# A cross-network kernel: half-size loads and earlier squares, and a block of its own for one difference of the first chunk pair

## The chip, the cores and the metric

The kernel runs on one core of a Trainium2 chip. The metric is the device time of one execution in microseconds (us). All data are float32.

## What is computed

The reference is a compressed interaction network of three layers over x (1024 examples, 64 fields, 16 embedding columns):

```python
for i in range(3):
    z = jnp.einsum('bfe,bge->bfge', x0, h)          # all products of a field with a row of h
    y = jnp.einsum('oc,bce->boe', Ws[i], z.reshape(Bn, f0 * fh, e)) + bs[i][None, :, None]
    x_i, h = (y[:, :64], y[:, 64:]) if i != 2 else (y, y)
    xs.append(x_i)
pooled = jnp.sum(jnp.concatenate(xs, axis=1), axis=2)
return pooled @ fc_w.T + fc_b
```

Everything after the second half of the first layer is linear in what it multiplies, so the kernel folds the last layer and the output weights into small matrices ahead of the main loop. What remains for each example and column is two quadratic forms of x: h, the second half of the first layer, and q, a folded form of the third and second. Their product, and a few linear terms, are summed.

## The kernel before, in words

**Tiling.** The batch is cut into 32 chunks of 32 examples, so a chunk has N = 32 x 16 = 512 columns. Fields lie on partitions. The products x_f x_g of a chunk come in 4 quarters j of 4 tiles i; a tile is 128 products x 512 columns, and a quarter, 128 x 2048, fills one of 14 SBUF blocks named z. A quarter is made by one VectorE product of xa (SBUF) with xp, a PSUM copy that ScalarE makes of the loaded xb (`second`, L563). A plain chunk contracts its 16 tiles with both weight matrices wh (for h) and wq (for q).

**Pairs.** Chunks 0 to 3 are the head, chunks 4 and 5 follow as plain chunks, 30 and 31 (and the q half of 2 and 3) end the kernel as plain ones. The other 24 chunks go in 12 pairs (n = 0 to 11, k = n + 3). A pair's two chunks a and b are multiplied by the two weight matrices in a scheme that needs seven runs of matmuls instead of eight, at the price of sums and differences. Each run has seven tiles, in two rows j = 0 (4 tiles) and j = 1 (3 tiles). The operands are X and B21 (products of chunk a), B22 and T3 (products of chunk b, T3 from the sum that `w_both`, L649, makes), and three differences that GpSimd makes, row by row (`w_mix`, L654): first T2 = T3 - X, then T3 = B22 - T2 in place, then T2 = T2 - B21 in place. Row j = 1 of T2 overwrites row 1 of X: its block is `p["X"][1]` (L657). Six of these GpSimd operations belong to a pair, on 128 x 2048 (row 0) or 128 x 1536 (row 1) elements.

**Windows.** TensorE works on one pair per window. The runs go into three PSUM banks: alpha in one half of the array's columns, delta and beta in the other. `window` (L738) writes the order out by hand as two columns of jobs that `zipped` (L530) interleaves, so that a job of one half runs beside a job of the other. Column one: the run X into alpha, jobs left over from the pair before (`first_fill`, 3 jobs), the run T2 into alpha, `second_fill` (2 jobs, and those handed over), the run T3 into alpha, 2 more jobs. Column two: the run T3 into delta, `late_run` of the pair before (10 jobs), the run B21 into beta, and the negative run, T2 (after its second difference) into delta. Of that last run the final `p["late"]` jobs are handed over to the next window: two from the first pair, then one and two in turn. Windows after the first read X row 1 ahead of row 0. The window of the first pair (n = 0, "window 0") is filled with jobs left of chunks 4 and 5 and with empty places (None). `squares` (L731) ends each window with four matmuls of 64 x 64.

**Order.** All is emitted in the order of times given to `at` (L527); T0 = 33 is window 0, SPAN = 31 the distance of windows, in places of TensorE's list and not in us. Each engine then works its own list in that order, and waits on semaphores where data or a buffer isn't ready. VectorE's list about window 0: X row 1 and B21 row 0 of the first pair (L645), `factors` of chunks 0 and 1 (L287 and L288: the second multiplies hb by a snapshot, both in SBUF, into uu), a sum (L299), B21 row 1, the products of the second pair up to its X row 1, among them `factors` of chunks 4 and 5 (L290), then the second pair's B21. Blocks z are handed out by `take` from a list of vacant ones, first freed first taken, each with a number of uses.

**Loads.** All loads are issued by SyncE in the same order. `load_e` (L160) brings x of a chunk to 128 partitions (the 64 fields twice), `square` (L169) squares the upper half in place on ScalarE. `h_extra` (L577) reads the squares, `v0x` (L584) the lower half, `q_extra` (L572) both. The first four chunks to be treated so are 4, 5, 0 and 1: loaded at 0, squared at 22, read at 28.1. `load_wx` (L542) loads two weight tables of 1 MB at -0.2 and -0.1; GpSimd weighs them (L548), VectorE adds them up (L552) and ScalarE places them (L557, at 17.1 and 20.1).

Of the kernel before, what the change touches and what calls it, by code (L numbers as in the profile page):

```python
# [38 lines left out]
AF = mybir.ActivationFunctionType  # L39
# [3 lines left out]
F = 64  # L43
# [25 lines left out]
def cin_kernel(ctx, tc, xra, xrb, wh, w0r, w1h, w2t, wx1, wx0, vec, out):  # L69
    nc = tc.nc  # L70
# [6 lines left out]
    halves = [slice(0, F), slice(F, 128)]  # L77

    def const_tile(name, shape):
        return const.tile(shape, F32, tag=name, name=name)  # L80
# [4 lines left out]
    def take(uses=1):  # L85
        n = vacant.pop(0)
        left[n] = uses
        return n

    def used(n, times=1):  # L90
        left[n] -= times
        assert left[n] >= 0
        if left[n] == 0:
            vacant.append(n)
# [22 lines left out]
    for base in (0, 64, -64):  # L117
        nc.gpsimd.affine_select(
            out=shift, in_=shift, compare_op=ALU.not_equal, fill=1.0, base=base,
# [12 lines left out]
    va, vb, v0 = (const_tile(n, [128, F]) for n in ("va", "vb", "v0"))  # L132
# [6 lines left out]
    xas, xbs, xxs, es = {}, {}, {}, {}  # L139
# [19 lines left out]

    def load_e(c):  # L160
        es[c] = sp.tile([128, N], F32, tag="e", name=f"e_{c}", bufs=4)
        nc.sync.dma_start(out=es[c], in_=xra[c, 0:128])

    def load_xx(k):
        xxs[k] = sp.tile([128, N], F32, tag="xx", name=f"xx_{k}")
# [1 line left out]
            nc.sync.dma_start(out=xxs[k][halves[n]], in_=xra[2 * k + n, 0:F])  # L167

    def square(c):  # L169
        nc.scalar.activation(es[c][halves[1]], es[c][halves[1]], AF.Square)  # L170

    def load_chunk(c):
        load_xa(c)
# [200 lines left out]
    for h in range(2):  # L374
        at = slice(32 * h, 32 * h + 32)
# [38 lines left out]
    def m_ap(f1, f2, dims):  # L414
        return bass.AP(tensor=md.tensor, offset=md.offset + f1 * row + f2 * F, ap=dims)
# [3 lines left out]
    for half, queue in enumerate((nc.sync, nc.scalar)):  # L419
        queue.dma_start(  # L420
            out=m_ap(0, 32 * half, [[row, F], [1, 32 * F]]), in_=m_rows[halves[half]]
# [5 lines left out]
        out=m_ap(64, 68, [[row, 4], [4 * F, 7], [1, 4 * F]]),  # L427
        in_=m_rows[0:4, 4 * F :].rearrange("p (k c) -> p k c", c=4 * F),
# [98 lines left out]
    def at(when, fn, *args, **flags):  # L527
        ops.append((when, len(ops), fn, args, flags))

    def zipped(when, *columns):  # L530
        for n, column in enumerate(columns):
            for m, job in enumerate(column):
                if job is not None:
                    at(when + m + n / len(columns), *job)
# [99 lines left out]
    def w_run(p, out, w, name, start=False, at_t=0, order=GROUPS):  # L634
        return [
            (w_job, p, out, w, j * NI + i + at_t, name, start and n == 0)
            for n, (j, i) in enumerate(order)
        ]

    wh_all, wq_all = w_all[:, :, 0:64], w_all[:, :, 64:128]  # L640
    s1, s2, s3, s4, neg = (ws[:, n] for n in range(5))
# [12 lines left out]
    def w_mix(p, j, out, in0, in1):  # L654
        p.setdefault(out, {})
        if j not in p[out]:
            p[out][j] = take(9) if j == 0 else p["X"][j]  # L657
        o, x, y = p[out][j], p[in0][j], p[in1][j]
        tiles = slice(j, NI)
        nc.gpsimd.tensor_tensor(  # L660
            blocks[o][:, tiles], blocks[x][:, tiles], blocks[y][:, tiles], ALU.subtract
        )
        for b in (x, y):
            if b != o:
                used(b)
# [26 lines left out]
    def make_pair(t, p, when, mixed):  # L692
        a, b = p["a"], p["b"]
        for when, c, j, name, uses in (
            (when[0], b, 2, "B22", 5), (when[1], b, 0, None, 0), (when[2], b, 0, "T3", 9),
            (when[3], a, 0, "X", 5), (when[4], b, 3, "B22", 6), (when[5], b, 1, None, 0),
            (when[6], b, 1, "T3", 9), (when[7], a, 1, "X", 12), (when[8], a, 2, "B21", 5),
            (when[9], a, 3, "B21", 6),
        ):
            if name is None:  # L700
                at(t + when, w_both, p, j)
                continue
            if name != "T3":
                at(t + when - (3.3 if p["k"] > 4 and name == "B22" and j == 2 else 2.7), second, c, j)
            at(t + when, w_product, p, c, j, name, uses)
        for when, j, *names in zip(
            mixed, (0, 1, 0, 1, 0, 1), *zip(
                *(2 * (("T2", "T3", "X"),) + 2 * (("T3", "B22", "T2"),) + 2 * (("T2", "T2", "B21"),))
            )
        ):  # L710
            at(t + when, w_mix, p, j, *names)

    def first_fill(p):
        a = p["a"]
        return [
            (w_job, p, beta, wq_all, NI, "X"), (w_job, p, beta, wq_all, NT - NI, "B21"),
            (lambda: q_extra(a, va, p["beta"]),),
        ]

    def second_fill(p):  # L720
        return [
            (w_job, p, delta, wh_all, NI, "X"), (w_job, p, delta, wh_all, NT - NI, "B21"),
        ] + w_run(p, delta, neg, "T2")[-p["late"] :]

    def late_run(p):
        b = p["b"]
        return [
            (w_job, p, alpha, neg, NI, "T3"), (w_job, p, alpha, s4, NI, "B22"),
        ] + w_run(p, alpha, s4, "B22") + [(lambda: q_extra(b, vb, p["alpha"]),)]
# [8 lines left out]
    def window(t, p, fill, late, pad=[], order=GROUPS[4:] + GROUPS[:4]):  # L738
        zipped(
            t,  # L740
            w_run(p, alpha, wq_all, "X", True, order=order) + fill[0] + w_run(p, alpha, s2, "T2")
            + fill[1] + w_run(p, alpha, s1, "T3")
            + [(w_job, p, alpha, wh_all, NI, "T3"), (w_job, p, alpha, s1, NI, "B22")],
            w_run(p, delta, s3, "T3", True) + late
            + w_run(p, beta, wq_all, "B21", True, 2 * NI)
            + pad + w_run(p, delta, neg, "T2")[: -p["late"]],
        )
        at(t + 30.2, squares, p)
        at(t + 6.8, snap_p1, p)
        at(t + 6.9, snap_p7, p)  # L750
        at(t + 6.8 + len(fill[0]) + 7, snap_u2, p)

    def end_pair(t, p, whens):
        hb_, qa, uub, ha, uua, xv, add = whens
        at(t + hb_, w_hb, p)
        at(t + qa, w_qa, p)
        at(t + uub, w_uu, p, alpha, "A", snaps[2])
        at(t + ha, w_ha, p)
        at(t + uua, w_uu, p, delta, "O", snaps[0])
        at(t + xv, x_v0x, p["k"])  # L760
        at(t + add, sums, p["k"])


    def load_pair(t, p, b0, a0, b1, a1):
        a, b = p["a"], p["b"]
        at(t + b0, load_xa, b)
        at(t + b0, load_xb, b, 2, 0)
        at(t + a0, load_xa, a)
        at(t + a0, load_xb, a, 0)
        at(t + b1, load_xb, b, 3, 1)  # L770
        at(t + a1, load_xb, a, 1, 2, 3)
        for c in (b, a):
            at(t + 1, load_e, c)
            at(t + 14, square, c)
        at(t + 1.1, load_xx, p["k"])
# [5 lines left out]
    at(-0.1, load_wx, 1, wx1)  # L781
    for n in (4, 5, 0, 1):
        at(0, load_e, n)
        at(22, square, n)
    for n in (0, 2):
        at(0.1, load_xx, n)
    for v, fc, mul, add, put in ((0, fcr[:, 0:64], 4, 17, 17.1), (1, fcr[:, 64:128], 5, 20, 20.1)):
# [32 lines left out]
    for n in range(NPAIR):  # L820
        k = n + 3
        s = k % 2
        p = {
            "k": k, "A": halves[s], "O": halves[1 - s], "b": 2 * k + s, "a": 2 * k + 1 - s,
            "late": 2 - n % 2,
        }
        pairs.append(p)
        t = T0 + SPAN * n
        if n == 0:
            load_pair(t, p, -39.9, -33.3, -33.05, -27)  # L830
            make_pair(
                t, p, (-23.4, -20.7, -20.4, -17.8, -14.2, -11.5, -8.1, -1, 0.5, 3),
                (-5, 6.6, 7.2, 12.4, 16.4, 21.7),
            )
            left5 = [[(contract_half, 5, 3, i, n) for i in (2, 3)] for n in range(2)]
            window(
                t, p, ([left5[1][0], (q_extra, 4, va)], [left5[1][1]]),
                [left5[0][0], (q_extra, 5, va), None, None], [left5[0][1], None, None, None, None],
                GROUPS,
            )  # L840
        else:
            q = pairs[-2]
            load_pair(t, p, -34, -28, -27.8, -27.7)
            make_pair(
                t, p, (-21.4, -18.7, -18.4, -15.8, -12.2, -9.5, -6.1, -2, 1.6, 4.2),
                (-5, 2.8, 7.2, 12.4, 16.4, 21.7),
            )
            window(t, p, (first_fill(q), second_fill(q)), late_run(q))
            end_pair(t, q, (0.7, 11.7, 17.9, 22.3, 23.2, 24, 27.5))
# [45 lines left out]
    c, k = NCH - 1, NP - 1  # L895
    t, q = T0 + SPAN * NPAIR, pairs[-1]
# [3 lines left out]
    for n, when in ((2, t - 4), (3, t - 4), (c - 1, t), (c, t)):  # L900
        at(when, load_e, n)
        at(t + 12, square, n)
# [9 lines left out]
    for n in (2, 3, c - 1, c):  # L912
        at(t - 0.1 + (n > 3) * 22, new_acc, n)
    qs = [[(head_q_half, n, m) for m in range(NT)] for n in (2, 3)]
    zipped(
        t,
        first_fill(q) + second_fill(q) + qs[0] + [(q_extra, 2, va), (q_extra, c - 1, va, None, True)],
        qs[1][:3] + late_run(q) + qs[1][3:] + [(q_extra, 3, va), (q_extra, c, va, None, True)],
    )
# [128 lines left out]
```

## Time and profile before

The time before is 467.2 us, the median of 3 runs (467.14 to 468.12). The profiled execution spans 468.5 us.

| engine | busy us | share of the span |
|---|---|---|
| TensorE, matmuls (PE) | 459.3 | 98% |
| TensorE, weight loads (PEld) | 171.1 | 37% |
| VectorE (DVE) | 397.1 | 85% |
| ScalarE (ACT) | 114.9 | 25% |
| GpSimd (POOL) | 330.3 | 71% |

How to read it: in a timeline a row has the start in us from the begin of the span, the time it covers in us, the engine, the line of the kernel, the operation, out<-in by the program's names, and how many are merged. In brackets stands the idle time of the engine ahead of it and what ended that. In the list of waits a row has who waited for whom, then the us in total, how many times, and the longest. DMA moves 91.29 MB in all, a mean of 195 GB/s; in the stretch ahead of window 0, from 52 to 75 us, it runs without pause.

### The profile page before, as it was taken

To read this page: it belongs to the slowest core of one execution; us is meant where nothing else is said; L and a number is where in the kernel's file an instruction comes from. 1 tells how busy PE (TensorE), PEld (TensorE's weight loads), DVE (VectorE), ACT (ScalarE), POOL (GpSimd) and SP (SyncE) were. 2 spreads that over 40 slices of the span, in tenths; PEclk is the share of its full clock that TensorE was granted. 3 is DMA by queue.
4 is the path that set the end of the run, shared out by engine and by line. 5 is a ranking of instruction groups with operands and counts; after the bars stand their busy time and mean duration, and the time that the engine had idled before them with its cause. 6 is when DMAs were issued, how large, how long until landed. Compare 5 with 4: busy or idle time off the path is not lost.

```text
span 468.5 us, 6050 instructions
## 1 busy us (share of the span) xinstructions
PE 459.3 (98%) x2308; PEld 171.1 (37%) x2308; DVE 397.1 (85%) x283; ACT 114.9 (25%) x211; POOL 330.3 (71%) x99
## 2 busy tenths in 40 slices
PE   7999999998999999999999999999999999999997
PEld 4565343232333333333333333333333333355444
DVE  3995597998898998989898998989898998999621
ACT  2142211441222213131312313122311314222101
POOL 5323689189997979899797979989797979600000
PEclk9999999999999999999999999999999999999999
DMA  8986999694818375562827465471828656061000
GB/s 301 401 289 153 355 414 297 217 313 146 290 50 277 127 235 190 162 243 90 303 70 248 167 205 207 140 279 63 307 81 252 219 174 231 24 224 46 0 1 2
DMA packets 35297, 91.29 MB, mean 195 GB/s; under 512 B 6240, under 2 KB 6912, under 8 KB 30340
## 3 DMA queue, kind: packets, MB, share of 16 engines
q1 hardware_dynamic: 34212, 89.88, 56.0%
q10 hardware_dynamic: 1056, 1.02, 0.8%
q8 instruction: 18, 0.29, 0.3%
q14 instruction: 11, 0.09, 0.1%
HBM read 89.25 MB, written 1.64 MB: 194 GB/s over the span
## 4 chain that ended last, share of the span: by engine, by line
PE 74%; DVE 12%; issue 6%; DMA 4%; POOL 3%; ACT 1%; SPq 1%; POOLq 0%; DVEq 0%; ACTq 0%
PE alpha L537 41%; PE acc L537 11%; PE beta L537 6%; DVE z L645 6%; PE delta L537 6%; PE acc L253 6%; PE acc L271 3%; POOL z L660 2%; DMA z<-in_wx 2%; DMA z<-in_w0r 2%; DVE acc L299 1%; POOL z L548 1%; DVE uu L688 1%; DVE xp L651 1%; DVE uu L295 1%
## 5 line engine op out<-in xcount | busy, mean ns | idle before, releaser
L660 POOL TENSOR_TENSOR z<-z,z 128x2048 f32<-128x2048 f32 x72 | 286.7, 4031 | 39.5 <-PE alpha L537 27.7
L645 DVE TENSOR_TENSOR z<-xa,xp 128x2048 f32<-128x2048 f32 x96 | 216.7, 2280 | 13.2 <-POOL z L660 12.2
L537 PE MATMUL alpha<-z,ws 128*64 128x512 f32 x576 | 196.6, 592 | 0.0
L537 PE MATMUL delta<-z,ws 128*64 128x512 f32 x336 | 150.7, 594 | 1.2 <-POOL z L660 1.2
L565 ACT COPY xp<-xb 128x512 f32<-128x512 f32 x93 | 54.7, 590 | 222.1 <-DVE z L645 167.1
L537 PEld LDWEIGHTS alpha<-z,ws 128*64 128x64 f32 x576 | 61.5, 137 | 105.1 <-issue 103.8
L537 PE MATMUL beta<-z,w_all 128*64 128x512 f32 x216 | 96.9, 593 | 0.0
L537 PE MATMUL alpha<-z,w_all 128*64 128x512 f32 x192 | 86.9, 595 | 0.9 <-DVE z L645 0.9
L537 PE MATMUL acc<-z,w_all 128*64 128x512 f32 (+3 forms) x320 | 78.0, 509 | 0.0
L239 DVE TENSOR_TENSOR z<-xa,xp 128x2048 f32<-128x2048 f32 (+2 forms) x33 | 67.5, 2087 | 8.7 <-ACT xp L565 5.3
L537 PEld LDWEIGHTS delta<-z,ws 128*64 128x64 f32 x336 | 45.0, 137 | 14.2 <-issue 11.4
L537 PEld LDWEIGHTS alpha<-z,w_all 128*64 128x64 f32 x192 | 25.3, 137 | 58.2 <-issue 48.8
L537 PEld LDWEIGHTS acc<-z,w_all 128*64 128x64 f32 (+1 forms) x320 | 33.2, 147 | 34.9 <-issue 33.8
L537 PEld LDWEIGHTS beta<-z,w_all 128*64 128x64 f32 x216 | 28.9, 137 | 13.9 <-issue 13.9
L253 PE MATMUL acc<-z,w_all 128*64 128x256 f32 x256 | 29.1, 382 | 2.6 <-DVE z L239 2.4
L239 POOL TENSOR_TENSOR z<-xa,xb 128x2048 f32<-128x2048 f32 x4 | 18.1, 4558 | 19.1 <-DMA xb<-in_xrb 19.1
L253 PEld LDWEIGHTS acc<-z,w_all 128*64 128x64 f32 x256 | 18.0, 137 | 14.8 <-DVE z L239 4.0
L537 PE MATMUL delta<-z,w_all 128*64 128x512 f32 x48 | 22.6, 592 | 0.0
L290 DVE SCALAR_TENSOR_TENSOR uu<-acc,vs,snap 64x512 f32<-64x512 f32 (+2 forms) x5 | 3.2, 643 | 20.3 <-ACT snap L282 20.2
L299 DVE TENSOR_REDUCE acc<-uu 128x64 f32<-128x1024 f32 (+3 forms) x20 | 20.2, 1017 | 0.2
L170 ACT ACTIVATE e<-e 64x512 f32<-64x512 f32 x32 | 18.3, 620 | 4.4 <-DMA e<-in_xra 4.0
L537 PE MATMUL y<-e,v 64*64 64x512 f32 x64 | 17.9, 613 | 0.0
(98 smaller groups left out, 290.0 us busy)
## 6 DMA issues: line engine op xcount, KB each, us to landing
xa<-in_xra SPq DMA_DIRECT2D x32, 1024.0 KB, 4.7
xb<-in_xrb SPq DMA_DIRECT2D x128, 256.0 KB, 6.9
e<-in_xra SPq DMA_DIRECT2D x32, 256.0 KB, 3.5
xx<-in_xra SPq DMA_DIRECT2D x32, 128.0 KB, 2.5
z<-in_w2t SPq DMA_DIRECT2D x2, 1024.0 KB
z<-in_wx SPq DMA_DIRECT2D x2, 1024.0 KB, 9.3
z<-in_w1h SPq DMA_DIRECT2D x1, 1024.0 KB
xa<-in_xra SPq DMA_DIRECT2D x3, 256.0 KB
```

The lines of the kernel that those rows point to most:

```text
L170: nc.scalar.activation(es[c][halves[1]], es[c][halves[1]], AF.Square)
L239: engine.tensor_tensor(blocks[zs[c, j]][:, at, :], xas[c][:, at, :], xbs[c][j].unsqueeze(1).to_broadcast([128, last - first, N]), ALU.mult,)
L253: nc.tensor.matmul(accs[c][halves[n]], w_all[:, t, 0:64], blocks[zs[c, j]][:, i, n * H2 : (n + 1) * H2], start=(t == 0), stop=(j == last a ...
L271: nc.tensor.matmul(accs[c][halves[1 - c % 2]], w_all[:, t, 64:128], blocks[zs[c, j]][:, i, :], start=(t == 0), stop=False, skip_group_chec ...
L295: nc.vector.scalar_tensor_tensor(uu[:, to, :], ys[k], cx, xxs[k], ALU.add, ALU.mult)
L299: nc.vector.tensor_reduce(acc[rows, of, k, half], uu[rows, of if at is None else at, E * half.start : E * half.stop].rearrange("p k (b e) ...
L537: nc.tensor.matmul(out, w, rhs, start=start, stop=stop, skip_group_check=True)
L548: nc.gpsimd.tensor_tensor(w, w, fc.unsqueeze(1).to_broadcast([128, 32, F]), ALU.mult)
L565: nc.scalar.copy(bank, xbs[c][j])
L645: nc.vector.tensor_tensor(blocks[b], xas[c], xbs[c][j].unsqueeze(1).to_broadcast([128, NI, N]), ALU.mult)
L651: nc.vector.tensor_tensor(bank, bank, xbs[p["b"]][j], ALU.add)
L660: nc.gpsimd.tensor_tensor(blocks[o][:, tiles], blocks[x][:, tiles], blocks[y][:, tiles], ALU.subtract)
```

## The change

It has three parts. First, `load_e` loads x to 64 partitions alone, half the bytes, and `square` reads that half and writes the other; the first four squares are emitted at 18 instead of 22, which is ahead of the second placement (20.1). The first pair's last loads of chunk b (quarters 3 and 1) are issued ahead of the second weight table. Second, the first pair's row 1 of T2 takes a block of its own instead of overwriting X row 1, and is emitted at 1.5 instead of 6.6. Third, the first pair hands no job of its negative run over; from the second pair on two and one are handed over in turn, and the empty places at the end of window 0 go from four to one. The purpose of the first part is that the squares are there when TensorE wants them, of the second that GpSimd need not wait for TensorE's reads of X, and of the third to fill the places that this opens.

```diff
     def load_e(c):
         es[c] = sp.tile([128, N], F32, tag="e", name=f"e_{c}", bufs=4)
-        nc.sync.dma_start(out=es[c], in_=xra[c, 0:128])
+        nc.sync.dma_start(out=es[c][halves[0]], in_=xra[c, 0:F])
...
     def square(c):
-        nc.scalar.activation(es[c][halves[1]], es[c][halves[1]], AF.Square)
+        nc.scalar.activation(es[c][halves[1]], es[c][halves[0]], AF.Square)
...
         if j not in p[out]:
-            p[out][j] = take(9) if j == 0 else p["X"][j]
+            p[out][j] = p["X"][j] if j and p["k"] > 3 else take(9 - 2 * j)
...
-            (when[6], b, 1, "T3", 9), (when[7], a, 1, "X", 12), (when[8], a, 2, "B21", 5),
+            (when[6], b, 1, "T3", 9), (when[7], a, 1, "X", 12 if p["k"] > 3 else 6), (when[8], a, 2, "B21", 5),
...
-        ] + w_run(p, delta, neg, "T2")[-p["late"] :]
+        ] + w_run(p, delta, neg, "T2")[7 - p["late"] :]
...
-            + pad + w_run(p, delta, neg, "T2")[: -p["late"]],
+            + pad + w_run(p, delta, neg, "T2")[: 7 - p["late"]],
...
     for n in (4, 5, 0, 1):
         at(0, load_e, n)
-        at(22, square, n)
+        at(18, square, n)
...
-            "late": 2 - n % 2,
+            "late": 1 + n % 2 if n else 0,
...
-            load_pair(t, p, -39.9, -33.3, -33.05, -27)
+            load_pair(t, p, -39.9, -33.3, -33.15, -27)
             make_pair(
                 t, p, (-23.4, -20.7, -20.4, -17.8, -14.2, -11.5, -8.1, -1, 0.5, 3),
-                (-5, 6.6, 7.2, 12.4, 16.4, 21.7),
+                (-5, 1.5, 7.2, 12.4, 16.4, 21.7),
             )
...
-                [left5[0][0], (q_extra, 5, va), None, None], [left5[0][1], None, None, None, None],
+                [left5[0][0], (q_extra, 5, va), None, None], [left5[0][1], None],
```

## The prediction

> **What bounds the kernel now.** I read the page first, then the idle time of TensorE, the stretches of one window each, and the timelines of VectorE and GpSimd around the first window. TensorE never lacks clock (9 tenths and over in every slice) and is busy 98%, so only its gaps and the order of its work can give time back. Part 1 and the list of waits:
>
> ```profile
> PE 459.3 (98%) x2308; PEld 171.1 (37%) x2308; DVE 397.1 (85%) x283; ACT 114.9 (25%) x211; POOL 330.3 (71%) x99
> ...
> POOL z L660 <- PE alpha L537: 27.7, 11, 3.1
> ...
> DVE z L645 <- POOL z L660: 12.2, 10, 1.6
> POOL z L660 <- PE delta L537: 11.8, 1, 11.8
> ...
> PE delta L537 <- POOL z L660: 1.2, 1, 1.2
> ...
> PE acc L537 <- ACT e L170: 1.0, 1, 1.0
> ```
>
> TensorE waits 1.0 us for a square (at 84.31) and 1.2 us for GpSimd (at 111.49); GpSimd waits 11.8 us for TensorE in the first window. These three are the change's targets. TensorE starts window 0 (n = 0) at 89.31, the next ones at 116.95, 143.87, 170.17. By stretches, columns as in the first line:
>
> ```profile
> core 0: us, PE busy (x) PEld busy (x) DVE busy (x) ACT busy (x) POOL busy (x), PEclk, DMA share, GB/s
> 89.31:116.95 27.64, 26.40 (x107) 8.36 (x103) 25.83 (x19) 9.23 (x16) 21.39 (x6) 1.00 0.73 242
> 116.95:143.87 26.92, 26.92 (x133) 8.74 (x129) 24.43 (x17) 6.33 (x11) 26.32 (x7) 1.00 0.55 188
> 143.87:170.17 26.30, 26.13 (x128) 8.45 (x124) 24.57 (x18) 5.88 (x11) 23.43 (x6) 1.00 0.55 183
> ```
>
> VectorE is nearly as full as TensorE: 25.83 of 27.64 us in window 0, so TensorE can't run ahead of it. Its timeline about window 0:
>
> ```profile
> 85.46 1.61 DVE L295 SCALAR_TENSOR_TENSOR uu<-y,cx,xx 128x512 f32<-128x512 f32 x2 [0.88 <-DMA xb<-in_xrb]
> ...
> 92.56 0.68 DVE L287 TENSOR_TENSOR hb<-acc,hb 64x512 f32<-64x512 f32 x1
> 93.27 0.69 DVE L288 TENSOR_TENSOR uu<-hb,snap 64x512 f32<-64x512 f32 x1
> 93.99 0.69 DVE L287 TENSOR_TENSOR hb<-acc,hb 64x512 f32<-64x512 f32 x1
> 94.72 0.69 DVE L288 TENSOR_TENSOR uu<-hb,snap 64x512 f32<-64x512 f32 x1
> ...
> 111.07 4.49 DVE L645 TENSOR_TENSOR z<-xa,xp 128x2048 f32<-128x2048 f32 x2
> 117.04 0.76 DVE L678 SCALAR_TENSOR_TENSOR snap<-alpha,vs,snap 64x512 f32<-64x512 f32 x1 [1.48 <-PE y L537]
> ```
>
> From 85.46 to 115.56 it has no gap. The last product there (ends 111.07 + 4.49 = 115.56) is X row 1 of the second pair, which window 1 reads first. GpSimd meanwhile stands still from 83.76 (79.20 + 4.56) to 95.56, and both L288 fall into that pause:
>
> ```profile
> 79.20 4.56 POOL L660 TENSOR_TENSOR z<-z,z 128x2048 f32<-128x2048 f32 x1
> 95.56 3.47 POOL L660 TENSOR_TENSOR z<-z,z 128x1536 f32<-128x1536 f32 x1 [11.81 <-PE delta L537]
> ```
>
> **What the Trainium skill says.** "SBUF — State Buffer", section "SBUF: two separate sides": VectorE and GpSimd share a port pair that is an exclusive lock for a whole instruction; a VectorE operation with two SBUF inputs takes it against a GpSimd operation that reads SBUF, and the later one blocks. L288 has two SBUF inputs (hb, snap); L645, L287, L651 and L295 have one operand in PSUM. The trace agrees in the only place where the two kinds meet, L494 with L512 and L513:
>
> ```profile
> 45.47 0.76 DVE L494 TENSOR_TENSOR w_all<-z 128x256 f32<-128x256 f32 x2 [2.38 <-DMA z<-md]
> 47.03 0.61 DVE L494 TENSOR_TENSOR w_all<-z 128x256 f32<-128x256 f32 x1 [0.81 <-DMA z<-md]
> 45.97 1.39 POOL L512 TENSOR_TENSOR ws<-w_all 128x512 f32<-128x512 f32 x1 [7.77 <-DVE w_all L494]
> 47.32 1.45 POOL L513 TENSOR_TENSOR ws<-ws,w_all 128x512 f32<-128x512 f32 x1
> 48.84 1.27 POOL L514 TENSOR_TENSOR ws<-w_all,ws 128x512 f32<-128x512 f32 x1
> ```
>
> The L494 that begins under L512 takes 0.61 us where one alone takes 0.42 (42.66) and ends 0.28 after L512's end (47.36); L513, behind it, takes 1.45 where L514 takes 1.27. So the waiting VectorE operation goes in between two GpSimd operations, and each pays. "TensorE: Matmul & The Clock Gate", Part 3 "Packing small matmuls — row/col tiling", says that matmuls on different tiles of the array run concurrently; the trace agrees: alpha and delta begin together every 0.43 us, two passes a job, so a pair of jobs, or one alone, costs 0.857 us.
>
> **Part 1: smaller e loads, squares at 18.** The loads move 128 KB in place of 256. The four squares now go to ScalarE after the first placement (77.08 + 0.47 = 77.55), take 2.19 us and end near 79.8, ahead of 82.24, where TensorE wants them; the wait of 1.0 us goes. The eight matmuls around it, now 82.24 to 86.68 = 4.44 us, need two rounds of four at 1.0 and 0.86 us (the four at 115.93 took 1.02). Saving 2.0 to 2.6, so window 0 starts at 86.7 to 87.3 on TensorE. VectorE gains less: its idle 0.88 at 85.46 (it waited for y) goes, so its whole run moves up 0.9. The two xb loads ahead of the second weight load delay that by about 0.5 MB / 0.4 MB per us = 1.3 us; GpSimd starts on it only at 74.7, behind its first weighing, so I cost this at nothing.
>
> **Part 2: T2 row 1 in its own block.** GpSimd no longer waits for TensorE's reads of X row 1; it starts when VectorE has made X row 1 (90.45 - 0.9 = 89.55). By 3.47 and 4.57 us in turn: T2 row 1 at 89.6 to 93.1, T3 row 0 to 97.6, T3 row 1 to 101.1, T2 row 0 to 105.6, row 1 to 109.1, in place of 114.9. TensorE's wait at 111.49 shrinks, and it could start window 1 at 112.7: negative run from 105.6, seven jobs x 0.857, 1.02 for the squares. But X row 1 of the second pair bounds that at 115.56 - 0.9 = 114.7. Blocks: by the order of takes and releases the extra block is one of the freed weight blocks, and the later takes get blocks whose readers are done microseconds before; no new wait.
>
> The cost lies with L288. It now starts at 93.27 - 0.9 = 92.37, under T2 row 1, which ends 93.07. By the L494 case the end is 0.28 + 0.27 (512 against 256 elements) = 0.55 after that: 93.6 in place of 93.06, +0.55. L287 follows to 94.35. T3 row 0 has begun behind the first L288, at about 93.5, and ends near 98.0, so the second L288 ends at 98.55 in place of 94.5: +4.05 in all. Behind it in VectorE's queue are the sums, B21 row 1 (ends 101.6; beta's last jobs wait some 2 us for it, absorbed by the later bound), and at the end X row 1 of the second pair: 115.56 - 0.9 + 4.05 = 118.7. Window 1 starts at 118.75 in place of 116.95: **+1.8 us**.
>
> **Part 3: nothing handed over by window 0.** A window's columns hold 28 + (jobs handed over to it) and 31 - (jobs it hands over). Before, windows 1, 3, ... have 30 and 30, even ones 29 and 29; now odd ones have 29 (the first 28 and 29), even ones 30. With 11 windows after the first, six are short instead of five. A long one takes 26.92, a short one 26.30, the rows above: -0.62. Short ones are bounded by VectorE (it waits for GpSimd until 6.4 us into the window, then works 19.8 us without gap: X row 1 ends at 26.26). The last window has no such successor, so TensorE's own 29 x 0.857 + 1.02 = 25.9 may stand: -0.97. I take -0.8. The tail after it has 24 or 25 jobs against 28: nothing.
>
> Sum: +1.8 - 0.8 = +1.0: 467.2 + 1.0 = **468.2 us**.
>
> **Rivals.** (a) No lock: L288 stays at 0.69. Window 1 at 114.7, -2.25, with -0.8 to -0.97: **464.1**, faster. For it: nothing else stands in the way; against it, L494's 0.61. Chance 0.16. (b) Partial: both only slow down while they overlap, L288 twice as long: +1.4 on VectorE, -0.85 - 0.8: **465.6**. L494's 0.19 us would fit that also. Chance 0.11. (c) GpSimd goes first each time: first L288 ends after T3 row 0 (98.2), the second after T3 row 1 (102.1), VectorE +7.6: **471.7**. Against it: L513 let L494 through. Chance 0.07. (d) The later weight load delays GpSimd's second weighing: needs over 2.5 us more than worked out; each us more comes on top, about **469**. Chance 0.04.
>
> **How the numbers follow.** My case has 0.62, spread 467.5 to 468.9 by the terms (0.9, 4.05, 0.62 to 0.97). It straddles the bound of slower at 468.1: of its 0.62, 0.39 slower and 0.23 same; with (c) and (d) slower is 0.50, same 0.23, faster 0.27 by (a) and (b). The range reaches over (a) and (b) and leaves out (c) and most of (d): 463.9 to 469.2.
>
> **What would show it.** Right: the two L288 at about 1.25 and 4.2 us; T2 row 1 on GpSimd at 89.6; no wait of TensorE for the square; one gap of some 5 us on TensorE ahead of window 1, ended by DVE z L645; odd windows of 26.3 and even ones of 26.9 us. Wrong: L288 at 0.69 (then a), or window 1 before 116.95. The odd windows still at 26.9 would undo part 3.

## The result

The changed kernel takes 473.51 us (472.02 to 473.58) where the kernel before takes 467.65 us (467.14 to 468.12) in the same comparison: a ratio of 1.0118, 95% interval 1.0093 to 1.0143. By that ratio it is slower by some 5.5 us (5.9 between the two medians), where 1.0 us had been forecast and the range ended at 469.2.

### The profile after

The lock came as the prediction had it, within 0.1 us. VectorE's timeline of the changed kernel about window 0 (start, us covered, then what runs):

```profile
79.46 2.29 DVE L552 TENSOR_REDUCE shift<-z 128x32 f32<-128x2048 f32 x1 [2.90 <-POOL z L548]
...
84.67 1.41 DVE L295 SCALAR_TENSOR_TENSOR uu<-y,cx,xx 128x512 f32<-128x512 f32 x2
...
91.56 0.68 DVE L287 TENSOR_TENSOR hb<-acc,hb 64x512 f32<-64x512 f32 x1
92.28 1.33 DVE L288 TENSOR_TENSOR uu<-hb,snap 64x512 f32<-64x512 f32 x1
93.64 0.69 DVE L287 TENSOR_TENSOR hb<-acc,hb 64x512 f32<-64x512 f32 x1
94.37 4.18 DVE L288 TENSOR_TENSOR uu<-hb,snap 64x512 f32<-64x512 f32 x1
...
114.22 4.49 DVE L645 TENSOR_TENSOR z<-xa,xp 128x2048 f32<-128x2048 f32 x2
```

The two L288 take 1.33 and 4.18 us instead of 0.69, and X row 1 of the second pair ends at 118.71 (114.22 + 4.49; forecast 118.7, though this match of two absolute times is luck, as the next section shows). But the first row shows something new: VectorE's second weighing sum waits 2.90 us for GpSimd. GpSimd's timeline says why:

```profile
67.51 4.54 POOL L548 TENSOR_TENSOR z<-z,vs 128x2048 f32<-128x2048 f32 x1 [1.12 <-DMA z<-in_wx]
74.88 4.55 POOL L548 TENSOR_TENSOR z<-z,vs 128x2048 f32<-128x2048 f32 x1 [2.83 <-DMA z<-in_wx]
...
89.60 24.68 POOL L660 TENSOR_TENSOR z<-z,z 128x1536 f32<-128x1536 f32 x6 [5.66 <-DVE z L645]
```

The second weight table had not landed when the first weighing was done: 2.83 us lost. And TensorE, by stretches from its last matmul of window 0 on (the clock is the third figure from the end), and then its first matmul of window 1:

```profile
core 0: us, PE busy (x) PEld busy (x) DVE busy (x) ACT busy (x) POOL busy (x), PEclk, DMA share, GB/s
113.65:118.76 5.11, 0.00 (x1) 0.01 (x1) 4.97 (x4) 0.61 (x2) 0.63 (x1) 0.77 0.26 77
118.76:121.00 2.24, 2.24 (x6) 0.77 (x8) 2.21 (x2) 0.56 (x1) 0.00 (x0) 0.50 0.93 345
121.00:123.00 2.00, 2.00 (x6) 0.48 (x4) 2.00 (x2) 0.59 (x1) 0.00 (x0) 0.50 0.88 266
...
118.76:147.11 28.35, 28.31 (x122) 8.80 (x123) 24.43 (x18) 6.31 (x12) 23.30 (x6) 0.92 0.53 181
147.11:174.03 26.92, 26.92 (x128) 8.74 (x129) 24.53 (x17) 6.94 (x12) 24.35 (x7) 1.00 0.54 186
174.03:200.20 26.17, 26.13 (x128) 8.45 (x124) 24.55 (x18) 5.75 (x11) 23.30 (x6) 1.00 0.51 168
...
118.76 1.12 PE L537 MATMUL alpha<-z,w_all 128*64 128x512 f32 x1 [5.11 <-DVE z L645]
```

The gap of 5.11 us, ended by VectorE's product, was forecast as a sign. What it does was not: during it the clock fell to a half, and window 1, forecast at 26.3 us, took 28.35. Windows 2 and 3 take 26.92 and 26.17, the order of long and short turned round as forecast.

### The two traces side by side

The first trace of the kernel before happens to have a late start: a load that VectorE's third product waits for lands 1.9 us later in it (the product starts at 8.56, after the change at 6.67, and VectorE's two before it stand alike). The comparison must therefore begin after the start. VectorE's first weighing sum (L552) serves as the mark: from it to the end of the span the kernel before takes 468.46 - 74.76 = 393.70 us, the changed one 471.74 - 72.08 = 399.66. The difference of 5.96 is what the timing shows (5.5, interval 4.3 to 6.7), and it splits so:

| stretch | before | after | difference |
|---|---|---|---|
| first sum to second sum (79.29; 79.46) | 4.53 | 7.38 | +2.85 |
| second sum to the first L295 (85.46; 84.67) | 6.17 | 5.21 | -0.96 |
| that to the end of X row 1 of the second pair | 30.10 | 34.03 | +3.93 |
| that to window 1 | 1.39 | 0.06 | -1.33 |
| window 1 | 26.92 | 28.35 | +1.43 |
| window 2 to the end | 324.59 | 324.63 | +0.04 |

The +1.43 of window 1 is 2.18 for the slow clock less 0.75 for its shorter list of jobs (26.17 instead of 26.92 us), as the experiments show.

### The profile page after: what moved, and what is told of

Same layout as the page of the kernel before. It is cut to its first block, busy times and chain, and to the rows that moved or that the text cites. A ratio compares the mean times of both kernels' runs of the same rounds, so it can differ in the third digit from the quotient of the medians.

```text
span 471.7 us, 6050 instructions
## 1 busy us (share of the span) xinstructions
PE 459.5 (97%) x2308; PEld 170.7 (36%) x2308; DVE 401.2 (85%) x283; ACT 114.4 (24%) x211; POOL 331.0 (70%) x99
## 3 DMA queue, kind: packets, MB, share of 16 engines
HBM read 85.05 MB, written 1.64 MB: 184 GB/s over the span
## 4 chain that ended last, share of the span: by engine, by line
PE 77%; DMA 10%; DVE 7%; SPq 3%; ACT 1%; issue 1%; DVEq 0%; ACTq 0%
PE alpha L537 50%; PE acc L537 9%; PE delta L537 7%; PE beta L537 7%; DMA xb<-in_xrb 5%; DVE z L645 4%; DMA e<-in_xra 3%; PE acc L253 2%; DMA z<-in_w0r 1%; DVE uu L288 1%; SPq L462 1%; DMA md<-z 1%; SPq L144 1%; SPq L423 1%; SPq L424 0%
## 5 line engine op out<-in xcount | busy, mean ns | idle before, releaser
L537 PE MATMUL delta<-z,ws 128*64 128x512 f32 x336 | 152.7, 601 | 0.0
L537 PE MATMUL alpha<-z,w_all 128*64 128x512 f32 x192 | 89.3, 608 | 5.7 <-DVE z L645 5.1
L537 PEld LDWEIGHTS acc<-z,w_all 128*64 128x64 f32 (+1 forms) x320 | 32.2, 147 | 35.2 <-issue 34.4
L651 DVE TENSOR_TENSOR xp<-xp,xb 128x512 f32<-128x512 f32 x24 | 16.8, 698 | 0.7
```

What stands on the lines that cost most here:

```text
L537: nc.tensor.matmul(out, w, rhs, start=start, stop=stop, skip_group_check=True)
L651: nc.vector.tensor_tensor(bank, bank, xbs[p["b"]][j], ALU.add)
```

## The experiments

All times of a trace are put against its own first sum, since its start differs from run to run. `psum` in a label means the L288 remedy, `wx` the old place of the weight table, `full` the e loads of 256 KB.

### The kernel before once more (before_again)

No edit.

> The kernel before once more, unchanged, for a second trace of it. The trace on record of before waited at its very start for a load (VectorE's product at 8.56 us; in the changed kernel the same product stands at 6.67 us), and was 1.9 to 2.7 us late from there on. Theory (the start of a run varies, and the trace on record had a late one): the product stands near 6.7, VectorE's weighing sum (L552, first) near 72, the second near 76.8, window 1 near 114, and the span near 465.5. Rival (the change itself made the start faster): all as on record, span near 468.5.

It took 468.67 us against 468.29, ratio 1.0007 (0.9996 to 1.0018). The third product stands at 7.95, the first sum at 72.72, the second at 77.25, window 1 at 114.90, the end at 466.43: 393.71 us from the first sum, as in the first trace (393.70). So the start varies, and the rest doesn't; the theory holds, though this start lies between the two and not, as forecast, beside that of the changed kernel. A forecast that puts absolute times of one trace against another is off by the start's luck: window 1 at 118.76 agreed with the forecast 118.75 only because 2.85 us of a new wait were offset by a start 2.68 us earlier.

### L288 with one SBUF operand (after_psum)

```diff
-                nc.vector.tensor_tensor(hc, acc_c[h], hc, ALU.add)
-                nc.vector.tensor_tensor(uu[h, 0, :], hc, q, ALU.mult)
+                nc.vector.tensor_tensor(acc_c[h], acc_c[h], hc, ALU.add)
+                nc.vector.tensor_tensor(uu[h, 0, :], acc_c[h], q, ALU.mult)
```

> The changed kernel, with L287 writing its sum back to PSUM and L288 reading it from there, so that L288 has one SBUF operand instead of two; nothing else. Theory (port lock of VectorE and GpSimd): L288 takes 0.69 us both times instead of 1.33 and 4.18, GpSimd's two operations 4.56 and 3.47 instead of 4.97 and 3.89; X row 1 of the second pair ends at 114.65 instead of 118.70; TensorE's gap ahead of window 1 falls from 5.1 to about 2 us and its clock stays at 1.0; the time falls by 4.05 + 2.2 to about 467.3. Rival (L288 was slow for its SBUF output or for the loads at that time, not for two SBUF inputs): still 4.2, time unchanged at 473.5.

467.53 us against 468.29, ratio 0.9985 (0.9971 to 1.0). VectorE's and GpSimd's timelines of this kernel:

```profile
92.57 0.68 DVE L288 TENSOR_TENSOR uu<-acc,snap 64x512 f32<-64x512 f32 x1
93.28 0.71 DVE L287 TENSOR_TENSOR acc<-acc,hb 64x512 f32<-64x512 f32 x1
94.02 0.69 DVE L288 TENSOR_TENSOR uu<-acc,snap 64x512 f32<-64x512 f32 x1
...
75.14 4.57 POOL L548 TENSOR_TENSOR z<-z,vs 128x2048 f32<-128x2048 f32 x1 [2.18 <-DMA z<-in_wx]
...
89.88 15.89 POOL L660 TENSOR_TENSOR z<-z,z 128x1536 f32<-128x1536 f32 x4 [5.66 <-DVE z L645]
```

GpSimd's four differences run without pause from 89.88 to 105.77, over both L288, and L288 takes 0.68 and 0.69. Same engine, same output of L288, same moment under GpSimd's work: one input moved from SBUF to PSUM removes the whole block, and the rival falls. From the first L295 to X row 1 it takes 29.92 (84.95 to 114.87) against 34.03. TensorE's gap ahead of window 1 shrinks to 1.87 us, and window 1 takes 26.17, which leaves no room for a slow clock. From the first sum to the end 392.74. What this kernel keeps is the wait for the table, here 2.18 us.

### TensorE kept busy through the gap (after_busy)

```diff
+    def keep_busy(p):
+        alpha(p)
+        for _ in range(5):
+            mm(delta(p), s3[:, 0], blocks[p["T3"][0]][:, 0, :], start=True)
...
+            if n == 1:
+                at(t - 0.4, keep_busy, p)
             window(t, p, (first_fill(q), second_fill(q)), late_run(q))
```

> The changed kernel with five more matmuls of 0.857 us each (the first job of the run T3 into delta, overwritten after) ahead of window 1, where TensorE had stood still for 5.1 us; they change no result. Theory (the still stand cost twice, since the clock fell to a half after it): the clock stays at 1.0, window 1 still starts at 118.8, the first seven pairs of jobs take 6.0 instead of 8 us, window 2 starts 26.3 us later instead of 28.35, and the time falls by about 2.1 to 471.4. Rival (window 1 is long for VectorE's wait for GpSimd at 127.4, whatever the clock): window 2 still 28.3 later, time unchanged or up.

472.79 us against 468.29, ratio 1.0099 (1.0084 to 1.0114). The timeline of its TensorE and its first two full windows:

```profile
115.17 4.50 PE L537 MATMUL delta<-z,ws 128*64 128x512 f32 x10
120.34 0.64 PE L537 MATMUL alpha<-z,w_all 128*64 128x512 f32 x1 [0.67 <-DVE z L645]
...
120.34:146.51 26.17, 26.13 (x122) 8.44 (x122) 24.43 (x18) 6.32 (x12) 23.30 (x6) 1.00 0.56 193
146.51:173.43 26.92, 26.92 (x128) 8.74 (x128) 24.53 (x17) 6.93 (x12) 24.49 (x7) 1.00 0.53 188
```

The idle 4.5 us are filled with work that is thrown away; the clock stays at 1.00, and window 1 takes 26.17 instead of 28.35. So 2.18 us of the loss are the clock's. VectorE's wait for GpSimd in window 1, which the rival held to be the reason, was its consequence: it is 3.36 us in the changed kernel and 1.18 us here, and GpSimd, for which it waits, waits in turn for TensorE's reads of X row 1. The time fell by less than the forecast 2.1 (ratios of 1.0118 and 1.0099 are 0.9 us apart, with intervals that overlap), so the timing alone doesn't show the price; the trace, put against the first sum, has 396.43 against 399.66, of which 1.05 is a shorter wait for the table (6.34 between the sums instead of 7.38) and 2.18 the clock.

### The weight table ahead of the two loads again (after_wx)

```diff
-            load_pair(t, p, -39.9, -33.3, -33.15, -27)
+            load_pair(t, p, -39.9, -33.3, -33.05, -27)
```

> The changed kernel with the two loads of quarters 3 and 1 back behind the second weight table (-33.05), nothing else. Theory (the table landed late behind them, and GpSimd and VectorE waited 2.8 and 2.9 us): GpSimd's second weighing starts with the end of the first, near 72.1, VectorE's second sum near 76.7, window 1 2.3 to 2.8 earlier, near 116.2; the gap ahead of window 1 stays over 4 us and the clock still falls; time about 471.0. Rival (other loads are as late, or the first pair's products then wait for quarter 3): window 1 still at 118.8, time 473.5.

472.65 us against 468.29, ratio 1.0085 (1.0064 to 1.0106). GpSimd weighs both tables in one go:

```profile
69.60 9.06 POOL L548 TENSOR_TENSOR z<-z,vs 128x2048 f32<-128x2048 f32 x2 [1.71 <-DMA z<-in_wx]
```

The sums follow each other at 74.17 and 78.69, 4.52 apart as in the kernel before. Window 1 starts 43.83 us after the first sum instead of 46.68, 2.85 earlier; its absolute time, 118.00, hides that under a late start. The gap is still 5.10 us and the clock still falls: window 1 takes 29.13 here, so the price of the clock isn't the same each time. From the first sum to the end: 397.58, which is 2.08 less than in the changed kernel: 2.85 for the table, less some 0.78 for the dearer clock. By the ratios the time fell by 1.5 us, with intervals that overlap; 2.5 had been forecast.

### Both remedies (psum_wx)

The two edits together.

> The changed kernel with both remedies so far: L288 reads its sum from PSUM, and the two loads of quarters 3 and 1 are back behind the second weight table. Theory (the lock costs 4.05 us and the late table 2.85, and nothing else of the change costs anything): from VectorE's first weighing sum to the end 389.9 to 390.9 us, against 393.7 in the kernel before, 399.7 in the changed one and 392.7 with the PSUM remedy alone; the time 2.8 to 3.8 us under the kernel before, a ratio of 0.992 to 0.994. Rival (the table is late for the e loads to 64 partitions, not for its place in the order): as with the PSUM remedy alone, 392.7 and a ratio of 0.9985.

465.80 us against 468.74, ratio 0.9935 (0.9921 to 0.9949): 0.65% faster than the kernel before, and faster than the changed one. From the first sum to the end 390.90, within the forecast. The first L295 comes 9.96 us after the first sum (10.70 before), L288 takes 0.68 and 0.69, and window 1 starts 40.11 after it (42.19 before) with a gap of 1.85 us on TensorE ahead of it:

```profile
112.04 0.64 PE L537 MATMUL alpha<-z,w_all 128*64 128x512 f32 x1 [1.85 <-DVE z L645]
...
112.04:138.22 26.18, 26.14 (x123) 8.44 (x123) 24.44 (x18) 6.33 (x12) 23.30 (x6) 1.00 0.59 197
```

This trace holds no record of the clock, so its 1.00 is no measurement; it is the length of window 1, 26.18 us, that shows no slow clock. This is the change as it was meant, with the lock and the late table out of the way, and it gains 2.8 us of the trace. What the earlier squares have in that was not run apart.

### Why the table was late (psum_full, psum_wx_full)

Two edits of the loads, with L288 from PSUM. In both the e loads go back to 128 partitions; psum_full keeps the changed order, psum_wx_full has the old one.

```diff
-        nc.sync.dma_start(out=es[c][halves[0]], in_=xra[c, 0:F])
+        nc.sync.dma_start(out=es[c], in_=xra[c, 0:128])
...
-        nc.scalar.activation(es[c][halves[1]], es[c][halves[0]], AF.Square)
+        nc.scalar.activation(es[c][halves[1]], es[c][halves[1]], AF.Square)
```

> The changed kernel with L288 reading PSUM, and with the e loads back to 128 partitions (256 KB) and the squares in place; the order of loads is the changed one, squares at 18. It tells whether the second weight table is late for its place in the order, or for the e loads behind it: 2 KB packets took 233 ns each while e went to 64 partitions, 85 ns with 128. Theory (slow packets of 64-partition loads hold the table's last packets up): the table lands 2 to 4 us after the first one instead of 7.5, GpSimd's second weighing follows the first at once, 389.9 to 391 us from the first sum to the end. Rival (its place in the order): the second weighing still waits 2.2 us or more, 392.7.

> As psum_wx, with the e loads to 128 partitions. Theory (64-partition loads save no time): not slower than psum_wx, 389.9 to 390.9 us from the first sum to the end, and the table lands a little sooner. Rival (half the bytes do help): 0.3 us or more slower than psum_wx.

psum_full: 466.09 us, ratio 0.9938 (0.9918 to 0.9958), 390.65 from the first sum. psum_wx_full: 465.60 us, ratio 0.9937 (0.992 to 0.9955), 390.91. Neither differs from psum_wx by what can be measured. GpSimd's weighing in psum_full, with the changed order:

```profile
67.26 9.21 POOL L548 TENSOR_TENSOR z<-z,vs 128x2048 f32<-128x2048 f32 x2 [1.15 <-DMA z<-in_wx]
```

9.21 instead of 9.06, so a wait of about 0.1. SyncE's timeline tells when the second table landed: its next loads go out as earlier ones land. Counted from the landing of the first table:

| e loads | table ahead of the two loads | table behind them |
|---|---|---|
| 128 partitions | 2.65 (before), 3.30 (before_again), 3.27 (part23), 3.40 (psum_wx_full) | 4.75 (psum_full) |
| 64 partitions | 2.54 (psum_wx_par), 3.19 (after_wx), 4.27 (psum_wx) | 6.41 (after_busy), 6.82 (after_psum), 7.48 (the change) |

psum_wx_par, described below, has the loads of psum_wx. GpSimd is through with the first table after 4.7 us, so only what lies beyond costs. The order alone adds 1.35 to 2.1, in one run, and just reaches the limit (worked out had been 1.3); the 64-partition loads alone add nothing that stands out of the spread of runs; together they bring the table to 6.4 to 7.5, and GpSimd waits 1.8 to 2.8 us. The expectation of psum_full was wrong in that the table came 4.75 and not 2 to 4 us after, and its rival was wrong too: neither cause is enough. That the table lands sooner with 128 partitions, as psum_wx_full was to show, is not shown. Window sums of the changed kernel, and of the kernel before in its second trace, over the same stretch:

```profile
66.00:70.00 4.00, 4.00 (x12) 1.57 (x12) 3.38 (x2) 0.59 (x1) 2.88 (x2) 1.00 1.06 393
70.00:74.00 4.00, 4.00 (x20) 1.40 (x22) 1.92 (x1) 0.00 (x0) 2.05 (x1) 1.00 1.06 147
```

```profile
66.00:70.00 4.00, 4.00 (x11) 1.72 (x10) 4.00 (x2) 0.15 (x1) 2.85 (x2) 1.00 0.99 402
70.00:74.00 4.00, 4.00 (x19) 1.24 (x18) 1.31 (x2) 0.59 (x1) 4.00 (x2) 1.00 1.06 357
```

The last two figures are the share of time in which the DMA engines were busy and what they moved. While e goes to 64 partitions they are as busy as ever (1.06) and move 147 instead of 357 GB/s. The two kernels differ in the order of loads too, but psum_full, with the changed order and 128 partitions, moves 390 from 70 to 72 us, where the changed kernel moves 151. "Half the bytes" is no less time. The median e load over the kernel, last figure, before and after:

```profile
e<-in_xra SPq DMA_DIRECT2D x32, 256.0 KB, 3.5
```

```profile
e<-in_xra SPq DMA_DIRECT2D x32, 128.0 KB, 4.1
```

The other traces spread widely: 3.8 to 4.7 us with 256 KB, 3.7 to 6.2 with 128 KB.

The Trainium skill says so on "SBUF — State Buffer", section "Door 1: The DMA port swizzle (why `[64,N]` ≈ `[32,N]`)": partitions 0 to 63 reach 8 of the 16 ports, and a transfer to them gets about half the rate. The traces agree in direction; the traffic of all loads together falls by more than half here.

### The block and the hand-over without the first part (part23)

The loads as before, squares at 22; the block of its own and the hand-over as changed.

```diff
-        at(18, square, n)
+        at(22, square, n)
...
-            load_pair(t, p, -39.9, -33.3, -33.15, -27)
+            load_pair(t, p, -39.9, -33.3, -33.05, -27)
```

(and the diff of psum_full on e loads; L288 as in the changed kernel)

> The changed kernel with all of its first part undone: e loads to 128 partitions, squares in place at 22, the loads' order of before. What is left is the block of its own and the jobs no longer handed over (the block can't be had without the latter: 14 blocks are too few). Theory (the lock makes the change slow on its own): L288 at 1.3 and 4.2 us, X row 1 of the second pair 4.0 us later than before counted from the first sum, a gap of 4 us or more ahead of window 1 and a clock of 0.5 after it; 398 to 399 us from the first sum to the end, the time 4.3 to 5.3 us over the kernel before, a ratio of 1.009 to 1.011. Rival (the earlier squares bring VectorE's and GpSimd's operations together): L288 at 0.69, no more than 393.7.

471.87 us against 468.74, ratio 1.0065 (1.0047 to 1.0083). VectorE's timeline and window 1:

```profile
90.62 1.33 DVE L288 TENSOR_TENSOR uu<-hb,snap 64x512 f32<-64x512 f32 x1
91.97 0.69 DVE L287 TENSOR_TENSOR hb<-acc,hb 64x512 f32<-64x512 f32 x1
92.70 4.19 DVE L288 TENSOR_TENSOR uu<-hb,snap 64x512 f32<-64x512 f32 x1
...
117.10:144.91 27.81, 27.77 (x122) 8.65 (x122) 24.43 (x18) 6.31 (x12) 23.30 (x6) 0.94 0.58 192
```

The block of its own, with the hand-over that goes with it, makes the kernel slower without the first part: the lock, X row 1 44.94 us after the first sum (40.80 before, +4.14), the gap of 5.08 us and the clock. From the first sum to the end 397.42, some 0.6 under what was expected, since the clock recovered sooner (window 1 takes 27.81); the ratio too is lower than the forecast 1.009 to 1.011. L288 takes 1.33 and 4.19 us with the squares at their old place, so the earlier squares have no part in the lock, and the rival falls.

### The old order of hand-over (psum_wx_par)

```diff
-            "late": 1 + n % 2 if n else 0,
+            "late": 2 - n % 2 if n else 0,
```

> psum_wx with the hand-over of the kernel before from the second pair on (one and two jobs in turn instead of two and one; the first pair still hands none over). Theory (a window with 30 jobs a column takes 26.92 us and one with 29 is bounded by VectorE at 26.17, so the changed order has one long window less, and the last window gains nothing, since its last matmuls wait for VectorE's reading of the bank y): odd windows 26.92, even ones 26.17 to 26.30, 391.3 to 391.7 us from the first sum to the end in place of 390.9, a ratio to before of 0.9945. Rival (the order of the hand-over makes no difference over the whole): 390.9.

466.33 us against 468.27, ratio 0.9958 (0.9945 to 0.9972), 391.33 from the first sum where psum_wx has 390.90. Its windows:

```profile
112.45:139.37 26.92, 26.92 (x124) 8.71 (x124) 24.41 (x17) 6.89 (x12) 23.90 (x6) 1.00 0.60 200
139.37:165.67 26.30, 26.13 (x128) 8.45 (x124) 24.57 (x18) 5.80 (x11) 23.43 (x6) 1.00 0.52 175
```

With 28 and 30 jobs in window 1 it is the long one again, so the length follows the longer column. The 0.43 us agree with the sign of the theory; the timing alone can't tell 0.4 us apart.

## Why the prediction was wrong, point by point

- **What bounds window 1: right for the changed kernel.** VectorE's gapless run to X row 1 of the second pair ends the gap there. In the kernel before it was TensorE itself, which was busy from 111.49 until 116.95, 1.39 us after X row 1; the change passes the bound from one to the other, as the prediction had it.
- **The lock: right.** The forecast was +0.55 us for the first L288 and +4.05 for both, from one L494 of 0.61 us in the trace and the lock that it took from the Trainium skill. Measured were +0.64 and +4.13, and VectorE's stretch grew by 3.93, since L295 took 0.20 less. Both L288 ended 0.55 us after the GpSimd operation under which they had begun (93.61 and 93.06, 98.55 and 98.00), as worked out. after_psum shows that it is the second SBUF operand.
- **The earlier squares: right.** VectorE's idle time at L295 is gone, 0.96 us against 0.9. TensorE gained less than the forecast 2.0 to 2.6: its window 0 starts 13.39 us after the first sum instead of 14.55, or 13.27 in psum_wx, where the table is not late. Nothing follows from that, since VectorE bounds window 1.
- **The hand-over: right in the windows, not at the end.** Short windows take 26.17, forecast 26.30, and there is one more of them, worth 0.75; the -0.97 for the last window did not come. There the jobs end early (squares at 411.44, window 11 from 386.40), but the matmuls into y start only after VectorE's last read of the pair before. The changed kernel's TensorE and VectorE:

```profile
412.39 1.08 PE L537 MATMUL y<-e,v 64*64 64x512 f32 x4
...
411.56 0.74 DVE L295 SCALAR_TENSOR_TENSOR uu<-y,cx,xx 128x512 f32<-128x512 f32 x1
```

  That y waits for the bank is argued from these times, and no run took it away. The -0.8, taken between -0.62 and -0.97, is near the measured -0.71 by luck.
- **First step that failed: "I cost this at nothing"**, of the second weight table. It cost 2.85 us. The 1.3 us for the place in the order was about right (1.35 to 2.1, in one run). Missing was what the smaller e loads do when the table goes out just ahead of them: with them it lands 1.7 to 2.7 us later still. The prediction had called them merely half the size. That they hold up the last of the table because all traffic slows down while they are in flight is argued from the rates; that it takes both, the order and the 64 partitions, is shown by psum_full and psum_wx. Rival (d) was this wait, with a chance of 0.04 and no cause named beyond the order. It set the room at 2.5 us beyond the 1.3, without saying from which landing; even in the old order and with 128 partitions the table lands 2.65 to 3.4 us after the first one, so of GpSimd's 4.7 us only 1.3 to 2.1 were left.
- **Second step that failed: the gap of some 5 us on TensorE ahead of window 1 had no price of its own.** Its clock fell to 0.50, and window 1 took 28.35 instead of 26.17: 2.18 us. The Trainium skill, "TensorE: Matmul & The Clock Gate", Part 1, section "HAM oscillation — how this bites in real kernels", warns of idle gaps over about 3.4 us. The runs agree: gaps of 5.1 us brought a fall (changed kernel, after_wx, part23), gaps of 1.8 to 1.9 did not (psum_full, whose clock is recorded at 1.00; after_psum and psum_wx by the length of window 1), and filled with dead work the gap costs nothing further (after_busy). No run has a gap of between 1.9 and 5.1 us ahead of window 1.

The terms that the prediction had came out at +0.93 (1.64 up to window 1, where 1.8 was forecast, and -0.71 from the windows instead of -0.8), close to its +1.0. With the two terms that it left out this is 0.93 + 2.85 + 2.18 = 5.96, which is what lies between the traces.

## What to carry to other kernels

Before an engine is let run earlier, ask which operations of its neighbours stood in the pause that it now fills: two L288 of 0.7 us each, harmless in a pause, cost 4 us under GpSimd's long operations, and one operand in PSUM gave all of it back. A gap on TensorE that lasts long enough (5.1 us here) has two prices, itself and the clock after it. Halving a load's bytes by halving its partitions made it no shorter, and slowed down the traffic around it. Two traces are compared from a mark behind their first loads, not from zero.

## What the runs showed of the hardware that wasn't expected

- In a gap of about 5.1 us without a matmul the clock falls, and is at 0.50 for the first 3.3 (part23), 4.4 (the change) and 6.0 us (after_wx) of work; the price was 1.64 us (part23, 27.81 - 26.17), 2.18 (the change) and 2.96 (after_wx) for the same gap, each time about half of the time at 0.50.
- While loads to 64 partitions are in flight, all traffic is slower: with e to 64 partitions the DMA engines moved 147 GB/s at full business (the change, 70 to 74 us), against 357 (before_again).
- The start of a run differs by up to 2.9 us at VectorE's first sum (71.83 in psum_full to 74.76 before), and in the one kernel that was traced twice nothing after it does: 393.70 and 393.71 us.
